# W_up for four pairs at a time by a two-level bilinear scheme of 49 block products, gate and lora_A as extra columns, part of the weight operands streamed

## The chip, the cores and the metric

The kernel runs on one core of a Trainium2 chip. TensorE (PE) multiplies matrices and writes into PSUM; VectorE (DVE) and ScalarE (ACT) read and write PSUM and SBUF; GpSimd (POOL) works in SBUF; SyncE (SP) only issues transfers here. The metric is the device time of one execution in microseconds (us), the median over several runs. Everything is float32.

## The reference

x has 128 samples of 64 channels by 1024. Two layers each add a branch to x:

```python
def _L0_cond_ref(x, embedding, ...):          # a 64x64 mix of the channels, its weights chosen per sample
    att = softmax(mlp(embedding)); agg_w = einsum('bk,koi->boi', att, weight); agg_b = att @ bias_k
    return einsum('boi,bih->boh', agg_w, x) + agg_b[:, :, None]
def _L0_ffn_ref(x, A, B, bias):               # rank 128
    return einsum('bsd,od->bso', x, A @ B.T) + bias
def _L1_cond_ref(x, c, weight, c_weight, bias):   # grouped convolution, 9 taps, 4 groups, plus a context
    return conv(x, weight) + (c @ c_weight.T)[:, :, None] + bias[None, :, None]
def _L1_ffn_ref(x, W_up, gate_w, expert_bias, lora_A, lora_B):
    top1 = argmax(x @ gate_w.T + expert_bias)                 # 4 experts
    z = einsum('nh,erh->ner', x, lora_A)                      # rank 8
    delta = the chosen expert's einsum('ner,ehr->neh', z, lora_B)
    return x @ W_up.T + delta                                 # W_up is 1024 x 1024
x = x + _L0_ffn_ref(_L0_cond_ref(x, ...), ...)
x = x + _L1_ffn_ref(_L1_cond_ref(x, ...), ...)
```

The change is about the last function: the product with W_up (8192 rows by 1024 by 1024), the gate and z.

## The kernel before

Two samples make a pair: 128 rows (partitions) of 1024. There are 64 pairs. The order of the instructions on every engine is the order of the program text.

- Layer 0 per pair: `layer0_in` (xt times B, 8 calls, line 401), `layer0_mix` (the sample's mix, lines 411 and 419), `layer0_out` (two matmuls of 512 columns, line 432, added to x by DVE, line 433). x then goes through DRAM (`x1d`) into the tile X, which holds it turned for the convolution.
- Convolution per pair: POOL makes differences of X (lines 469 and 470), `shared_in` (line 477) and `conv_in` (line 515) multiply, `shared_out` and `conv_out` (lines 492, 495, 527) add the context and write `yt`, which is the turned input of the W_up product: 8 blocks of 128 columns of the 1024 for each of the two pairs.
- W_up, two pairs at a time: the product is cut into 2 row blocks (pairs) x 4 x 4 blocks of 256, which would be 32 block products. A bilinear scheme does it with 26. `ffn_sums` has POOL make 17 sums of parts of yt (line 216). `products` runs the 26 block products (line 559): each is two matmul calls, 128 x 128 by 128 x 256, onto half of one of four PSUM banks `pb`. Between them, ACT and DVE copy, add or evict parts of these banks (lines 564 to 578), as the table `PRODUCTS` says. All 26 weight operands lie in SBUF (`W`), made at the start from W_up by 31 sums (`w_sums`, on DVE with ACT copies to PSUM, and POOL).
- Gate and lora: `gate_in` multiplies yt by gate_w and lora_A (16 calls, line 586), the result is transposed (line 598), `gate` picks the expert on DVE (lines 601 to 612), `turn` transposes the masked z (line 622), `lora` adds z times lora_B onto the four open banks (line 631), and `results` adds the banks to x (line 637) and stores the pair.
- The main loop runs over d, two pairs, 32 times. In it the products of d stand between layer 0 and the convolution of later pairs. Loads of x and xt are issued by POOL (lines 157 and 161), all other steady transfers by SP.

Of the kernel before, what the change touches and what calls it, by code (L numbers as in the profile page):

```python
# [45 lines left out]
NG = NPAIR // GP  # L46
# [9 lines left out]
QC = NC // 4  # L56
# [3 lines left out]
GT = 64  # L60
NX = 3
NBD = 3
# [3 lines left out]

Y_SUMS = (  # L70
    (4, "+", 5), (0, "-", 8), (9, "+", 1), (2, "-", 10), (4, "-", 7), (0, "-", 12), (3, "-", 13),
    (2, "+", 14), (6, "-", 15), (16, "-", 5), (12, "-", 15), (17, "-", 18), (11, "-", 8), (20, "-", 19),
    (21, "+", 7), (7, "-", 13), (21, "+", 3),
)
W_SUMS = (
    (10, 8, "-", 10), (16, 10, "-", 6), (17, 4, "n", 16), (2, 2, "-", 6), (18, 11, "-", 15),
    (19, 18, "n", 16), (3, 3, "n", 15), (20, 1, "-", 3), (21, 7, "-", 20), (21, 5, "n", 21), (18, 8, "+", 18),
    (1, 5, "-", 1), (5, 9, "-", 10), (10, 6, "+", 20), (10, 5, "+", 10), (20, 12, "+", 2), (22, 4, "-", 3),
    (23, 5, "-", 13), (7, 4, "+", 7), (24, 3, "+", 2), (24, 0, "-", 24), (9, 9, "-", 13), (25, 12, "-", 18),
    (0, 0, "-", 4), (0, 12, "+", 0), (4, 14, "-", 23), (4, 2, "+", 4), (13, 13, "+", 21), (11, 11, "-", 21),  # L80
    (11, 8, "+", 11), (12, 14, "-", 12),
)
PRODUCTS = (
    (2, 6, 8, 1, 0, (("copy", 0, "-"),)),
    (4, 10, 17, 1, 3, (("x", 4, "+"),)),
    (6, 11, 16, 1, 3, (("copy", 1, "+"),)),
    (2, 12, 2, 0, 4, (("x", 6, "+"),)),
    (6, 2, 19, 0, 6, (("add", 0, "+"),)),
    (5, 8, 3, 0, 7, (("add", 4, "-"),)),
    (3, 17, 21, 0, 10, (("x", 7, "+"), ("x", 1, "+"))),  # L90
    (0, 15, 18, 0, 11, (("x", 7, "+"),)),
    (5, 5, 1, 0, 12, (("x", 7, "-"),)),
    (7, 8, 10, 0, 15, ()),
    (7, 19, 5, 0, 15, (("x", 1, "+"), ("x", 5, "+"))),
    (2, 13, 20, 0, 16, (("x", 2, "+"),)),
    (1, 20, 6, 0, 16, (("x", 2, "-"),)),
    (4, 9, 22, 0, 17, (("add", 2, "-"),)),
    (6, 18, 15, 0, 17, (("copy", 7, "-"), ("copy", 3, "-"))),
    (1, 21, 23, 0, 18, (("copy", 6, "-"),)),
    (4, 1, 7, 0, 19, (("x", 1, "-"), ("x", 3, "+"))),  # L100
    (2, 0, 24, 0, 21, (("dcopy", 4, "+"), ("x", 0, "+"))),
    (6, 22, 9, 0, 22, (("x", 5, "-"),)),
    (0, 14, 25, 0, 23, (("copy", 2, "+"),)),
    (4, 23, 0, 0, 25, ()),
    (6, 7, 4, 0, 27, ()),
    (1, 10, 10, 0, 27, ()),
    (1, 24, 13, 0, 28, ()),
    (7, 16, 11, 0, 30, ()),
    (2, 3, 12, 0, 31, ()),
)  # L110
NW = 26
ON_POOL = (16, 19, 20, 21, 23, 24, 27, 28)
LAST = ((21, 2), (24, 0), (25, 3), (26, 1))
# [5 lines left out]
def block(ctx: ExitStack, tc: tile.TileContext, a: dict, out: bass.AP):  # L119
    nc = tc.nc  # L120
    const = ctx.enter_context(tc.tile_pool(name="const", bufs=1))
    xpool = ctx.enter_context(tc.tile_pool(name="xpool", bufs=8))
    xtp = ctx.enter_context(tc.tile_pool(name="xtp", bufs=3))
    ps = ctx.enter_context(tc.tile_pool(name="ps", bufs=4, space=PSUM))
    psb = ctx.enter_context(tc.tile_pool(name="psb", bufs=1, space=PSUM))
# [3 lines left out]
    bcp = ctx.enter_context(tc.tile_pool(name="bcp", bufs=3))  # L129
    z0p = ctx.enter_context(tc.tile_pool(name="z0p", bufs=2))  # L130
    cvp = ctx.enter_context(tc.tile_pool(name="cvp", bufs=1))
    ytp = ctx.enter_context(tc.tile_pool(name="ytp", bufs=2))
    sp = ctx.enter_context(tc.tile_pool(name="sp", bufs=2))
    sums = ctx.enter_context(tc.tile_pool(name="sums", bufs=1))
# [18 lines left out]
    xs, xts, bds, aggbs, ctxs = {}, {}, {}, {}, {}  # L153

    def load_turned(pr, eng):
        xts[pr] = xtp.tile([P, NC, P], F32, tag="xt", name=f"xt{pr}")
        eng.dma_start(xts[pr], a["xt"][pr])

    def load_rest(pr, eng):
        xs[pr] = xpool.tile([P, L], F32, tag="x", name=f"x{pr}")  # L160
        eng.dma_start(xs[pr], a["x"][pr])

    def load_x(pr, eng=nc.gpsimd):
        load_turned(pr, eng)
        load_rest(pr, eng)

# [7 lines left out]
    pk = const.tile([P, PK[-1]], F32, name="pk")  # L174
    nc.sync.dma_start(pk[:, : PK[4]], a["pk"][:, : PK[4]])
    nc.sync.dma_start(pk[:, PK[4] :], a["pk"][:, PK[4] :])
    condT, w0, b0, b1, w1, w2, b2, cwT, fs, ebias = (pk[:, f:t] for f, t in zip(PK, PK[1:]))
# [3 lines left out]
    nc.scalar.activation(warm, warm, AF.Gelu)  # L181
    bk = loaded("bias_k", [8, CH])
# [4 lines left out]
    W = const.tile([P, NW, QC, NQ], F32, name="w")  # L187
    wdone = [0]

    def load_w(k, eng):  # L190

        eng.dma_start(W[:, 4 * k : 4 * k + 4].rearrange("p j c n -> p (j c n)"), a["wq"][k])

    def w_sums(upto, aside=True):

        for k in range(wdone[0], upto):
            to, x, op, y = W_SUMS[k]
            fresh = [W_SUMS[j][0] for j in range(max(k - 2, 0), k)]
            if op != "-" and x in fresh:
                x, y = y, x  # L200
            first = W[:, x]
            if k in ON_POOL:
                combine(nc.gpsimd, W[:, to], first, op, W[:, y])
                continue
            if aside and x not in fresh:
                first = bank(f"pw{k}")
                nc.scalar.copy(first, W[:, x].rearrange("p c n -> p (c n)"))  # L207
                first = first.rearrange("p (c n) -> p c n", c=QC)
            combine(nc.vector, W[:, to], first, op, W[:, y])
        wdone[0] = max(wdone[0], upto)  # L210

    def combine(eng, to, x, op, y):
        if op == "n":
            eng.scalar_tensor_tensor(to, x, -1.0, y, ALU.mult, ALU.subtract)
        else:
            eng.tensor_tensor(to, x, y, ALU.add if op == "+" else ALU.subtract)  # L216
# [10 lines left out]
    ones = const.tile([P, P], F32, name="ones")  # L227
# [10 lines left out]
    aggd = dram.tile([NB, CH, CH], F32, name="aggd")  # L238
    ctxd = dram.tile([NB, CH], F32, name="ctxd")
# [23 lines left out]

    def mlp(w, h, b, name):
        p = bank(f"p{name}")
        nc.tensor.matmul(p[:, :NB], w, h, start=True, stop=True)
        o = const.tile([P, NB], F32, tag=name, name=name)
        nc.scalar.activation(o, p[:, :NB], AF.Gelu, bias=b)
        return o

    def spare(j, name):

        return psb.tile([P, N], F32, tag=f"pb{j}", name=name)
# [6 lines left out]
    def condition():  # L280
# [18 lines left out]
        nc.vector.reciprocal(rs, sm)  # L299
        nc.vector.tensor_scalar(att[:, :, :8], ex.unsqueeze(1).to_broadcast([P, 4, 8]), rs, None, ALU.mult)  # L300
# [6 lines left out]
    def b_row():  # L307

        p = spare(2, "pbs8")
        for c in range(NC):  # L310
            nc.tensor.matmul(p[:8, :P], ones[:, :8], bt[:, c], start=c == 0, stop=c == NC - 1)
        nc.scalar.copy(bs8, p[:8, :P])
# [16 lines left out]
    def own_bias(pr):  # L329

        mv[pr] = sums.tile([8, 2, CH], F32, tag=f"s{10 + pr}", name=f"mv{pr}")
        for b in range(2):
            nc.scalar.activation(mv[pr][:, b], bk, AF.Copy, scale=attT[:8, 2 * pr + b : 2 * pr + b + 1])

    def own_bd(pr):
        bdx[pr] = sums.tile([P, 2, CH], F32, tag=f"s{14 + pr}", name=f"bdx{pr}")
# [28 lines left out]
    def agg_all():  # L365

        to = aggd.rearrange("b i o -> b (i o)").rearrange("b (j h n) -> h b j n", j=4, h=2)
        for h in range(2):
# [4 lines left out]
            else:  # L373
                whole = W[:, NW - 4 :].rearrange("p j c n -> p j (c n)")
# [19 lines left out]
    xbs, z0s, yts, opened = {}, {}, {}, {}  # L394
    diffs, pms, m2s, pcs, zgs, ys = {}, {}, {}, {}, {}, {}
# [10 lines left out]
    def layer0_mix(pr):  # L406
        g, t = pr // GP, pr % GP
        own = pr < FIRST
        pz = bank(f"pz{pr}")
        bd = bdx[pr] if own else bds[g][:, t]  # L410
        nc.tensor.matmul(pz[:, :P], xbs.pop(pr), bd.rearrange("p b o -> p (b o)"), start=True, stop=not own)  # L411
# [3 lines left out]
        if own:  # L415
# [122 lines left out]

    def ffn_sums(d, first=0, end=len(Y_SUMS)):

        if not first:
            ys[d] = [yts[d][:, t, QC * k : QC * (k + 1)] for t in range(2) for k in range(4)]
        y = ys[d]
        for k, (u, op, v) in list(enumerate(Y_SUMS))[first:end]:
            y.append(sums.tile([P, QC, P], F32, tag=f"s{k}", name=f"s{k}_{d}"))
            combine(nc.gpsimd, y[-1], y[u], op, y[v])

    def part(d, r):
        return opened[d][r // 2][:, r % 2 * NQ : (r % 2 + 1) * NQ]

    def products(d, first, end):
        if not first:
            opened[d] = [psb.tile([P, N], F32, tag=f"pb{i}", name=f"pb{i}_{d}") for i in range(4)]
        for r, u, w, new, _, then in PRODUCTS[first:end]:
            p = part(d, r)
            if new == 2:
                nc.vector.memset(p, 0.0)
            for c in range(QC):
                nc.tensor.matmul(  # L559
                    p, ys[d][u][:, c], W[:, w, c], start=new == 1 and c == 0, stop=c == QC - 1, skip_group_check=True  # L560
                )
            for kind, to, op in then:
                if kind == "dcopy":
                    nc.vector.tensor_copy(part(d, to), p)
                elif kind == "copy" and op == "+":
                    nc.scalar.copy(part(d, to), p)
                elif kind == "copy":
# [231 lines left out]
    for d in range(NPAIR // 2):  # L799
# [8 lines left out]
        if d:  # L808
            zm = gate(d)
# [135 lines left out]
```

## Time and profile before

| | |
|---|---|
| median of 3 runs | 1276.93 us (1276.56 to 1277.66) |
| span of the profiled execution | 1275.4 us |
| PE busy | 1256.2 us, 98% |
| POOL, DVE, ACT busy | 731.1 us 57%; 698.4 us 55%; 233.2 us 18% |
| matmul instructions | 9255 |
| transfers | 189.72 MB, mean 149 GB/s; HBM read 118.90 MB, written 69.27 MB |
| SP's queue, POOL's queue, ACT's queue | 126.07 MB, 35.8% of 16 engines; 58.73 MB, 13.8%; 3.41 MB, 0.8% |
| share of the ending chain by line 559 (products) | 55% |

The profile is one execution, whose own time is the span. Busy time of PE counts instructions that overlap; the distance from one start to the next is the time that one takes of the engine. A float32 matmul call leaves two records.

### The profile page before, as it was taken

To read this page: it belongs to the slowest core of one execution; us is meant where nothing else is said; L and a number is where in the kernel's file an instruction comes from. 1 tells how busy PE (TensorE), PEld (TensorE's weight loads), DVE (VectorE), ACT (ScalarE), POOL (GpSimd) and SP (SyncE) were. 2 spreads that over 40 slices of the span, in tenths; PEclk is the share of its full clock that TensorE was granted. 3 is DMA by queue.
4 is the path that set the end of the run, shared out by engine and by line. 5 is a ranking of instruction groups with operands and counts; after the bars stand their busy time and mean duration, and the time that the engine had idled before them with its cause. 6 is when DMAs were issued, how large, how long until landed. Compare 5 with 4: busy or idle time off the path is not lost.

```text
span 1275.4 us, 23721 instructions
## 1 busy us (share of the span) xinstructions
PE 1256.2 (98%) x9255; PEld 1057.1 (83%) x9255; DVE 698.4 (55%) x1477; ACT 233.2 (18%) x586; POOL 731.1 (57%) x868
## 2 busy tenths in 40 slices
PE   8989999999999999999999999999999999999998
PEld 6768888888888888888888888888888888888886
DVE  6666545546545456555455555455555465455454
ACT  3321121111111111111211111111111111211111
POOL 2475676555576455676555676555775555765332
PEclk9989999999999999999999999999999999999999
DMA  9965444565444565444664444664444654445301
GB/s 307 341 164 160 147 136 115 147 176 163 135 131 111 165 176 161 140 118 110 176 176 149 143 110 128 176 174 143 137 109 141 176 171 135 137 113 149 104 34 67
DMA packets 184159, 189.72 MB, mean 149 GB/s; under 512 B 17392, under 2 KB 156656, under 8 KB 183536
## 3 DMA queue, kind: packets, MB, share of 16 engines
q1 hardware_dynamic: 166912, 126.07, 35.8%
q0 software_dynamic: 16128, 58.73, 13.8%
q10 hardware_dynamic: 1008, 3.41, 0.8%
q8 instruction: 74, 1.21, 0.4%
q14 instruction: 37, 0.30, 0.1%
HBM read 118.90 MB, written 69.27 MB: 148 GB/s over the span
## 4 chain that ended last, share of the span: by engine, by line
PE 93%; DMA 4%; DVE 1%; ACT 1%; issue 0%; SPq 0%; POOL 0%; DVEq 0%; POOLq 0%; ACTq 0%
PE pb L559 55%; PE pxb L401 9%; PE pd L432 8%; PE pc L515 8%; PE pm L477 4%; PE pg L586 4%; PE pb L631 3%; DMA w<-in_wq 1%; DMA x1d<-x 1%; PE pz L411 1%; DMA aggd<-agg 1%; DMA X<-x1d 1%; DMA ffn_bias<-in_ffn_bias 1%; ACT pw L207 0%; DVE yt L527 0%
## 5 line engine op out<-in xcount | busy, mean ns | idle before, releaser
L559 PE MATMUL pb<-w,s 128*128 128x256 f32 x2432 | 558.3, 380 | 6.0 <-DVE w L216 4.5
L559 PEld LDWEIGHTS pb<-w,s 128*128 128x128 f32 x2432 | 460.4, 191 | 72.1 <-DVE w L216 4.9
L469 POOL TENSOR_TENSOR df<-X 128x512 f32<-128x512 f32 x62 | 64.1, 1034 | 387.8 <-DMA X<-x1d 387.8
L559 PE MATMUL pb<-w,yt 128*128 128x256 f32 x896 | 225.6, 380 | 2.3 <-DVE x L637 1.8
L492 DVE TENSOR_TENSOR m<-pm,cx 64x512 f32<-64x512 f32 x124 | 85.3, 688 | 203.0 <-PE pm L477 196.4
L559 PEld LDWEIGHTS pb<-w,yt 128*128 128x128 f32 x896 | 162.9, 190 | 31.5 <-issue 8.7
L576 DVE TENSOR_TENSOR x<-pb,x 128x256 f32<-128x256 f32 x320 | 129.2, 421 | 95.6 <-PE pb L559 88.9
L216 POOL TENSOR_TENSOR s<-yt,s 128x256 f32<-128x256 f32 x224 | 165.6, 739 | 17.8 <-PE pb L559 2.8
L656 POOL TENSOR_TENSOR x<-x,ffn_bias 128x1024 f32<-128x1024 f32 x61 | 142.7, 2355 | 17.0 <-DMA x<-in_x 17.0
L401 PEld LDWEIGHTS pxb<-B,xt 128*128 128x128 f32 x1024 | 118.7, 194 | 25.1 <-DVE yt L527 22.0
L527 DVE TENSOR_TENSOR yt<-pc,m 128x512 f32<-128x512 f32 x124 | 122.6, 1112 | 25.0 <-ACT m L495 19.4
L401 PE MATMUL pxb<-B,xt 128*128 128x128 f32 x1024 | 124.6, 280 | 0.2 <-DMA xt<-in_xt 0.2
L432 PE MATMUL pd<-AT,z 128*128 128x512 f32 x256 | 121.3, 595 | 2.6 <-DVE attx L327 1.6
L515 PE MATMUL pc<-ws,df 128*64 128x128 f32 x1984 | 113.6, 273 | 0.0
L515 PEld LDWEIGHTS pc<-ws,df 128*64 128x64 f32 x1984 | 109.4, 137 | 0.0
L433 DVE TENSOR_TENSOR x<-pd,x 128x512 f32<-128x512 f32 x128 | 88.2, 691 | 37.4 <-PE pd L432 30.1
L571 ACT COPY v<-pb 128x256 f32<-128x256 f32 x96 | 35.8, 372 | 371.7 <-PE pb L559 352.9
L216 POOL TENSOR_TENSOR s<-s,yt 128x256 f32<-128x256 f32 x128 | 93.5, 731 | 15.7 <-PE pzt L622 8.3
L495 ACT COPY m<-m 64x512 f32<-64x512 f32 x124 | 76.6, 618 | 134.1 <-DVE m L492 124.5
L216 POOL TENSOR_TENSOR s<-s,s 128x256 f32<-128x256 f32 x128 | 92.2, 730 | 5.0
L578 DVE SCALAR_TENSOR_TENSOR x<-pb,x 128x256 f32<-128x256 f32 x128 | 54.0, 422 | 68.1 <-PE pb L559 66.6
L637 DVE TENSOR_TENSOR x<-pb,x 128x512 f32<-128x512 f32 x124 | 76.8, 683 | 8.7 <-PE pb L631 8.7
(107 smaller groups left out, 915.3 us busy)
## 6 DMA issues: line engine op xcount, KB each, us to landing
x1d<-x SPq DMA_DIRECT2D x128, 256.0 KB, 4.4
X<-x1d SPq DMA_DIRECT2D x128, 256.0 KB, 4.3
out<-x SPq DMA_DIRECT2D x62, 512.0 KB, 3.6
xt<-in_xt POOLq DMA_DIRECT2D x56, 512.0 KB, 6.0
x<-in_x POOLq DMA_DIRECT2D x56, 512.0 KB, 6.5
cx<-ctxd SPq DMA_DIRECT2D x32, 128.0 KB, 4.3
w<-in_wq SPq DMA_DIRECT2D x4, 1024.0 KB, 12.4
ab<-aggbd SPq DMA_DIRECT2D x30, 128.0 KB, 3.4
```

The lines of the kernel that those rows point to most:

```text
L216: eng.tensor_tensor(to, x, y, ALU.add if op == "+" else ALU.subtract)
L401: nc.tensor.matmul(pxb[:, :P], xt[:, c, :], bt[:, c, :], start=(c == 0), stop=(c == NC - 1))
L432: nc.tensor.matmul(pd, z0, at[:, cols], start=True, stop=True)
L433: nc.vector.tensor_tensor(x[:, cols], pd, x[:, cols], ALU.add)
L492: nc.vector.tensor_tensor(by_group(m2[half, b]), by_group(pm[half]), context(pr, b, half), ALU.add)
L495: nc.scalar.copy(m2[other, b], m2[half, b])
L515: nc.tensor.matmul(pc[o * H : (o + 1) * H, cols], diffs[pr][:, 2 * g + b, o], ws[:, g, o], start=True, stop=True,)
L527: nc.vector.tensor_tensor(yt.rearrange("m q (o g two) -> m two g q o", two=2, g=NGC)[:, b], by_group(pcs.pop((pr, b))), context(pr, b) if ...
L559: nc.tensor.matmul(p, ys[d][u][:, c], W[:, w, c], start=new == 1 and c == 0, stop=c == QC - 1, skip_group_check=True)
L576: nc.vector.tensor_tensor(x, p, x, ALU.add)
L637: nc.vector.tensor_tensor(x[:, cols], b, x[:, cols], ALU.add)
L656: eng.tensor_tensor(xs[pr], xs[pr], fbias, ALU.add)
```

## The change

W_up is now done for four pairs at a time, 16 times. Four pairs are two "rows" r of two pairs. The product is cut into 2 x 2 x 2 large blocks, which a bilinear scheme of 7 products handles (`Outer`, i = 0 to 6: operand sums `OPERANDS`, destinations `DESTS`). Each of the 7 is again cut into 2 x 2 x 2 and done with 7 products, in a form whose sums are chained (`inner`, `rest`). So there are 49 block products of two calls each, where 64 would be the plain number.

- Operands on the left: `gather` makes one sum of 1024 elements for five of the seven outers, `inner` makes four sums of 256 for each, all on POOL.
- Operands on the right: four of each outer's seven are held in SBUF (28); the other three (21 in all) are written to DRAM at the start (`w_store`) and fetched again for each group of four pairs (`w_fetch`, 768 KB, on ACT's queue) into a ring of two buffers.
- Gate: for outers 0 to 3 the held operands are 292 columns wide; the 36 last columns are gate_w and lora_A, brought through the same scheme. ACT copies these columns out of PSUM (`gated`), `gate` adds them up. The matmuls of `gate_in` and one transpose are gone.
- PSUM: one bank `pa` and a ring of three banks `pt` in place of the four `pb`. Every outer's results are evicted at once onto x, to one or two places.
- `lora` writes four banks of its own, which DVE adds to x.
- x for two pairs lies in one tile (4 tiles in place of 8), loaded and stored by transfers of 1 MB. All loads are issued by SP; POOL issues none. Buffers change: 2 BD in place of 3, 2 context buffers in place of 3, 3 yt in place of 2, and a 1024-byte scratch for POOL's transfers.
- The start is written out anew: the operands are formed by `w_block` and `w_late` between the first four pairs' products.

```diff
-Y_SUMS = (
...
-PRODUCTS = (
...
+DESTS = (
+    ((0, 1, "+"), (1, 1, "+")),
+    ((0, 0, "-"), (0, 1, "+")),
+    ((0, 0, "+"), (1, 0, "+")),
+    ((1, 0, "+"), (1, 1, "-")),
+    ((0, 0, "+"), (1, 1, "+")),
+    ((0, 0, "+"),),
+    ((1, 1, "+"),),
+)
+OPERANDS = (
+    ((0, 0),),
+    ((0, 0), "+", (0, 1)),
+    ((1, 1),),
+    ((1, 0), "+", (1, 1)),
+    ((0, 0), "+", (1, 1)),
+    ((0, 1), "-", (1, 1)),
+    ((1, 0), "-", (0, 0)),
+)
...
+    def w_fetch(i):
+        nc.scalar.dma_start(ring_tile(i).rearrange("p k c n -> p (k c n)"), wd[i])
...
+        def gather(self):
+            o = OPERANDS[self.i]
+            if len(o) == 1:
+                self.S = self.operand(*o[0])
+                return
+            self.S = sums.tile([P, GP, 4, P], F32, tag="S", name=f"S{self.name}")
+            combine(nc.gpsimd, self.S, self.operand(*o[0]), o[1], self.operand(*o[2]))
...
+        def product(self, p, lhs, w, fresh=False):
+            for c in range(2):
+                nc.tensor.matmul(p, lhs[:, c], w[:, c], start=fresh and c == 0, stop=c == 1, skip_group_check=True)
...
+        def first(self):
+            self.t1 = pst.tile([P, N], F32, tag="pt", name=f"ta{self.name}")
+            self.product(self.t1[:, : self.n], self.unit(0, 0), held(self.i, 0), True)
+        def spread(self):
+            self.pa = psa.tile([P, N], F32, tag="pa", name=f"pa{self.name}")
+            nc.scalar.copy(self.pa[:, :NQ], self.t1[:, :NQ])
+            self.gated(2, self.t1)
+        def rest(self, then, hooks):
+            self.t2 = pst.tile([P, N], F32, tag="pt", name=f"tb{self.name}")
+            wt = WT[self.i]
+            self.product(self.t2[:, :NQ], self.s[0], wt[:, 1], True)
+            v = tmp.tile([P, NQ], F32, tag="v", name=f"v{self.name}")
+            nc.scalar.copy(v, self.t2[:, :NQ])
+            hooks("a")
+            self.product(self.pa[:, :NQ], self.s[1], wt[:, 2])
+            nc.scalar.copy(self.t2[:, :NQ], self.pa[:, :NQ])
+            hooks("b")
+            self.product(self.t1[:, : self.n], self.unit(0, 1), held(self.i, 1))
+            self.gated(0, self.t1)
+            self.evict(self.t1[:, :NQ], 1)
+            hooks("c")
+            self.product(self.pa[:, :NQ], self.s[3], wt[:, 0])
+            hooks("d")
+            self.product(self.t2[:, : self.n], self.s[2], held(self.i, 2))
+            nc.scalar.copy(self.pa[:, NQ:], self.t2[:, :NQ])
+            both = self.pa.rearrange("p (k n) -> p k n", k=2)
+            combine(nc.vector, both, both, "+", v.unsqueeze(1).to_broadcast([P, 2, NQ]))
+            self.evict(both, 3)
+            if then:
+                then.first()
+            self.product(self.t2[:, : self.n], self.unit(1, 1), held(self.i, 3))
+            if then:
+                then.spread()
+            self.gated(1, self.t2)
+            self.evict(self.t2[:, :NQ], 2)
...
+    for d in range(1, ND):
...
+        w_fetch(1)
+        if more:
+            load_cond(r0)
+            load_cond(r1)
+            load_rows_of(r0)
+            load_turned(pairs(r1)[0])
+        q[1].gather()
+        q[1].inner()
+        if more:
+            for pr in pairs(r0):
+                add_fbias(pr, nc.gpsimd)
+        q[0].rest(q[1], nothing)
+        if more:
+            in_rows(r0)
...
+        w_fetch(6)
+        if more:
+            load_context(r1)
+        q[6].gather()
+        q[6].inner()
+        q[5].rest(q[6], nothing)
+        lora(d, 1, zts[1])
+        store(d, 0)
+        if more:
+            w_fetch(0)
+            for pr in pairs(r1):
+                differences(pr)
+            o[d + 1, 0].gather()
+            o[d + 1, 0].inner()
+        q[6].rest(o[d + 1, 0] if more else None, nothing)
+        store(d, 1)
+        if more:
+            conv_rows(r1)
```

The parts left out of the loop stand in the same manner: outer 1, then `out_rows(r0)`; outer 2, then `in_rows(r1)` and `lora(d, 0)`; outer 3, then `out_rows(r1)`; outer 4, then `conv_rows(r0)`. The fetch for outer k + 1 always stands before the `rest` of outer k.

## The prediction, made before the changed kernel was run

> **What bounds the kernel now.** I read four views in this order: the engines over 40 slices, the chain of work that ended last, TensorE's timeline over one period, and the groups of instructions.
>
> ```profile
> PE   8989999999999999999999999999999999999998
> PEclk9989999999999999999999999999999999999999
> ...
> PE 93%; DMA 4%; DVE 1%; ACT 1%; issue 0%; SPq 0%; POOL 0%; DVEq 0%; POOLq 0%; ACTq 0%
> 610.60:649.20 38.60, 38.60 (x288) 32.66 (x287) 20.85 (x45) 6.73 (x17) 22.97 (x27) 1.00 0.51 147
> ```
> TensorE (PE) works without a gap at full granted clock from about 100 to 1200 us. The last line is one period, two pairs in 38.53 us: PE 100%, VectorE (DVE) 20.85 us, ScalarE (ACT) 6.73, GpSimd (POOL) 22.97, DMA share 0.51. So a change is worth the PE time it removes, as long as no other engine or transfer becomes late.
>
> ```profile
> 594.45 1.97 PE L477 MATMUL pm<-wsum,X 128*64 128x128 f32 x32
> 596.25 1.92 PE L586 MATMUL pg<-yt,gl 128*64 128x128 f32 x32
> 597.99 3.66 PE L515 MATMUL pc<-ws,df 128*64 128x128 f32 x64
> 601.59 1.14 PE L631 MATMUL pb<-lb,zt 32*128 32x512 f32 x8
> 602.66 3.84 PE L401 MATMUL pxb<-B,xt 128*128 128x128 f32 x32
> ...
> 610.01 1.88 PE L432 MATMUL pd<-AT,z 128*128 128x512 f32 x4
> 611.73 0.38 PE L411 MATMUL pz<-bd,xb 128*128 128x128 f32 x2
> ...
> 617.40 12.95 PE pb L559 x60
> ```
> The first seven lines are the timeline (start, us), the last is from the chain. PE overlaps its instructions, so a price is the distance from one start to the next: pm 1.80 for two pairs, gate pg 1.74, convolution pc 3.60, lora 1.07, pd 1.72 per pair (4 records of 512 columns, 430 ns each). A block product's record of 256 columns costs 12.95/60 = 215.8 ns. Each matmul call leaves two records.
>
> ```profile
> L576 DVE TENSOR_TENSOR x<-pb,x 128x256 f32<-128x256 f32 x320 | 129.2, 421 | 95.6 <-PE pb L559 88.9
> L433 DVE TENSOR_TENSOR x<-pd,x 128x512 f32<-128x512 f32 x128 | 88.2, 691 | 37.4 <-PE pd L432 30.1
> L527 DVE TENSOR_TENSOR yt<-pc,m 128x512 f32<-128x512 f32 x124 | 122.6, 1112 | 25.0 <-ACT m L495 19.4
> L571 ACT COPY v<-pb 128x256 f32<-128x256 f32 x96 | 35.8, 372 | 371.7 <-PE pb L559 352.9
> L656 POOL TENSOR_TENSOR x<-x,ffn_bias 128x1024 f32<-128x1024 f32 x61 | 142.7, 2355 | 17.0 <-DMA x<-in_x 17.0
> q0 software_dynamic: 16128, 58.73, 13.8%
> out<-x SPq DMA_DIRECT2D x62, 512.0 KB, 3.6
> aggd<-w SPq DMA_DIRECT2D x1, 1024.0 KB, 5.9
> x<-in_x ACTq DMA_DIRECT2D x1, 512.0 KB, 11.0
> ```
> These are prices of the small work that the new scheme adds, and of transfers.
>
> **The change, on PE, per four pairs (two old periods, 77.06 us).** 52 calls per two pairs become 98 per four: 208 records become 196, so 12 x 0.2158 = -2.59. The gate matmuls go: 2 x 1.74 = -3.48; with them two transposes pgt at 0.11 = -0.22. Added: 4 of the 7 outer products carry 36 extra columns in 4 of their 7 inner ones, 4 x 4 x 2 calls x 2 = 64 records. From 256 to 512 columns a record grows 215.8 to 430 ns, 0.84 ns a column, so 30 ns each: +1.92. Lora and its transposes keep their number. Net -4.37: **a new period of 72.7 us**.
>
> **What must stay hidden, per new period.** DVE: 24 evictions of 256 columns x 0.421 = 10.1, 12 of 512 x 0.69 = 8.3, 7 sums in PSUM x 0.69 = 4.8, lora 8 x 0.68, pd 8 x 0.69, yt 8 x 1.11, m 8 x 0.69, z 1.4, two gates of ten small operations, 4: together 54 us against 41.7. POOL: 5 gathers of 1024 elements x 2.36, 28 sums x 0.74, bias 9.4, differences 8.3: 50 us against 46. ACT: 28 copies x 0.37, 12 gate copies of 36 columns (about 0.25, as zg), m, xb, zt: 20 us, and 7 fetches to issue. All are below 72.7.
> The order matters more than the sums. I walked one period by hand, T = 0 at the first inner product of outer 0. PE: outers 0 to 2 6.52 each (3 x 0.863 + 4 x 0.983), outer 3 6.40, 4 and 5 6.04, 6 6.16; between them stand in order in_rows 3.8, out_rows 3.4, in_rows and lora 4.8, out_rows 3.4, convolution 5.4, lora 1.1, convolution 5.4. The tightest circle inside an outer runs from its fifth product: ACT copy 0.37, DVE sum 0.69, two evictions 1.38, ACT spread 0.37, then the next outer's second product may start: 2.8 us with hops of some 0.04 (DVE w ended at 68.46, PE began at 68.50). PE has 0.98 + 0.98 + 0.86 = 2.8 us of its own there plus the work in between, at least 1.07. Hidden. If DVE runs late there, the delay shows one to one. POOL finishes each outer's sums 6 us or more before use, because their two buffers come free one outer earlier.
>
> **The streamed operands.** 105 fetches (15 periods x 7) of 768 KB on ACT's queue, 82.6 MB, and 5.5 MB of stores. q0 moved 58.73 MB in 13.8% of the span, 334 GB/s, so this takes 264 us more of all 16 engines: share 0.51 to about 0.75. A fetch is issued by ACT between its copies; it blocks nothing long, since its ring buffer is already free. From issue to the matmul that needs it I count 6.7 us (outer 6: issued after the m copies, covered by outer 5 and lora alone), then 10.0 (1), 10.2 (2), 11 (4), 12.4 (0), 14.8 (3), 14.9 (5). Price of landing, not in the trace for this size: below, between 512 KB in 3.6 and 1024 KB in 5.9, so 4.7; above, the 512 KB load on ACT's queue that took 11.0 while the DMA share was near 1. I take near the lower end, 5 to 6, because the share is 0.75 and the packets are long; 0.3 us a period is put in for bad cases, 4 us in all.
> The Trainium skill speaks against taking ACT's queue as a path of its own: "DMA: Bandwidth & Descriptors", section "Issuing engines are not separate DMA queues", says all queues run on the same 16 engines and interleave. If SP's queue takes every second turn, the fetch needs its 2.4 us at 334 GB/s twice: 7.1 instead of 4.7, so 0.4 late for outer 6, 6 us over 15 periods, in place of my 4.
> All x and xt loads move from POOL's to SP's queue, where they queue with x1d, X, stores and conditions: 32 issues of about 0.55 = 18 us per period, and X and x have 10 us or more to spare in my walk. POOL loses its issues and its wait for `out<-x` (41.1 us in all), which cost PE nothing.
>
> **The start.** Before, lora of the second period ends at 139.2. The changed kernel reaches the same point (eight pairs convolved, four finished) at: 44.2 (pd of pair 3, as before) + 79.0 of PE work (seven outers 45.2, three convolution groups 16.2, the rest 17.6) = 123.2 without a wait. I expect waits of 12.8: 1.4 for W's first block (4 DVE steps behind ACT copies), 1.0 in its first outers, 4.3 where outer 3's gather waits for four yt sums and then POOL's 2.36, 0.5 there, 4.0 where lora wants PSUM banks while DVE still works off block 2 and pd, 1.6 in outer 3 to 5. So 136. Bounds: 123 with none, 149 with twice as many.
>
> **The end.** The last period has no new pairs: 72.7 less 26.1 of in, mix, out and convolution, less 0.98 = 45.6; without work between outers the circle above shows at four places, 1.5 in all. After the last matmul: eviction 0.42, then one store of 1 MB (5.9) instead of 256 KB pieces: 6.5 against some 4 before.
>
> **Sum.** 136 + 14 x 72.7 + 45.6 + 1.5 + 4 + 6.5 = 1211.4 us of span. The profile before had 1275.4, the median of the runs 1276.93, so 1.5 lie around it: **1213 us**, a factor of 0.950.
>
> **Rivals.**
> (a) *The gain is there, half is eaten by short waits per period*: DVE, 54 us in 72.7 and in strict order, is late in the circle or with PSUM banks (lora wants four at once), or the start takes 149. For it: in the walk DVE has hardly a pause from T = 12 to 29 and 43 to 58, and margins of 1 us. Against: no step of the walk is late. With 2 us a period, 28, and 10 at the start: about 1250.
> (b) *The fetches become the bound, slower than before.* A landing time of L costs (L - 6.7) + (L - 10.0) + (L - 10.2) a period. The gain of 64 us is gone at 4.3 us a period, from L = 10.4. For it: the 11.0 above, and 12.4 for 1 MB in the start. At 11.0 it is 6.1 a period, 92 us: about 1305. Against: both rows lie where the DMA share was 0.9 to 1.0; in the steady part, loads of 512 KB on a queue of their own took 6 to 6.5 even behind one another.
> (c) *The gate columns save nothing*, if 36 columns more cost as much as a record of 128 (118 ns): 64 x 0.118 = 7.6 instead of 1.9, 5.6 x 16 = 90 us, 1303. Two records of a matmul with 256 and 512 columns lie on one line, so I give this little.
>
> **Chances.** Forecast 0.66 (its own range 1201 to 1226), (a) 0.22, (b) 0.09, (c) 0.03. A measurement of this kernel can tell 0.2%, 2.6 us. Faster: the forecast and (a), less a tail: 0.87; within 0.2%: 0.02; slower: 0.11. The range 1201 to 1255 takes the forecast and most of (a).
>
> **What would show it.** The changed period: 72.7 us with 196 records for the products, 64 of them near 246 ns; no idle PE there. Idle PE in front of products that read the streamed tiles would be (b), with fetches landing above 10 us; idle in front of the second product of an outer, released by ACT, would be (a). A start that reaches the fourth convolution group later than 149, or DVE busy above 85% in a period, would make the prediction wrong.

## The result, and the profile after

| | before | after |
|---|---|---|
| median | 1276.74 us (1275.59 to 1277.66, 4 runs) | 1414.38 us (1409.36 to 1414.79, 4 runs) |
| span of the profiled execution | 1275.4 us | 1413.0 us |
| PE, DVE busy | 98%, 55% | 89%, 71% |

The ratio is 1.1068 (95% interval 1.1045 to 1.109): slower by a tenth, where a gain of 5% was forecast, and outside the range. The page of after, the rows that answer to those of before (busy shares, slices, the chain by engine):

```profile
PE 1253.7 (89%) x8007; PEld 994.8 (70%) x8007; DVE 1004.8 (71%) x1670; ACT 316.8 (22%) x928; POOL 784.6 (56%) x746
...
PE   8879899898997979979899898989989899798997
...
PEclk9989989999999989999999999999999999999999
...
PE 53%; issue 14%; DVE 11%; POOL 10%; DMA 8%; SPq 1%; ACT 1%; ACTq 0%; DVEq 0%; POOLq 0%
```

PE now has dips all along the span, and DVE and POOL stand in the chain, where they had 1% and 0%. 1248 matmul records are gone, yet the end comes later. One new period, from one `in_rows` to the next but one (columns: length; busy us of PE, weight load, DVE, ACT, POOL; clock; DMA share; GB/s):

```profile
616.10:701.47 85.37, 76.67 (x496) 61.00 (x495) 60.73 (x99) 18.20 (x54) 48.73 (x45) 0.96 0.63 196
```

85.4 us instead of the 72.7 of the prediction: PE is idle for 8.7 us and the mean granted clock is 0.96. In the kernel before, PE was busy for all of the 38.60 us of a period (two pairs). Where PE stands still is in its timeline (start, us, then the wait and its releaser in brackets):

```profile
601.43 1.03 PE L645 MATMUL pa<-wt,s 128*128 128x256 f32 x4
602.29 1.15 PE L645 MATMUL ta<-wg,yt 128*128 128x292 f32 x4
609.45 0.48 PE L736 MATMUL pzt<-ident,zm 128*128 128x128 f32 x1 [6.01 <-DVE xr L505]
609.72 1.91 PE L645 MATMUL pa<-wt,s 128*128 128x256 f32 x4
611.43 2.15 PE L645 MATMUL tb<-wg,s 128*128 128x292 f32 x4
613.38 1.90 PE L645 MATMUL ta<-wg,S 128*128 128x292 f32 x4
```

The transpose `pzt` of `turn` needs a PSUM bank that `pd` still holds, since DVE has not yet added `pd` to x (L505). The products behind it then take about 1.9 us in place of 1.03 to 1.15: the granted clock from 609.72 to 616.10 is 0.59. The same place one row later (637.10) waits 2.72, and here the products behind it stay at 1.03. That is not so in every period: behind five of the 14 waits of this second kind the clock fell too, as behind the one that ended at 203.97:

```profile
609.72:616.10 6.38, 6.38 (x18) 4.69 (x18) 4.11 (x8) 0.62 (x2) 1.88 (x3) 0.59 0.71 171
637.10:642.00 4.90, 4.90 (x39) 4.21 (x41) 4.77 (x10) 0.91 (x3) 1.66 (x2) 1.00 0.57 163
204.00:209.00 5.00, 5.00 (x16) 4.13 (x17) 4.26 (x8) 0.62 (x2) 0.60 (x1) 0.66 0.54 161
```

What made DVE late, on DVE and below it on POOL:

```profile
601.25 0.45 DVE L718 TENSOR_TENSOR sc<-lg,mx 128x8 f32<-128x8 f32 x1
601.74 2.28 DVE L719 TENSOR_TENSOR sc<-sc,rank 128x8 f32<-128x8 f32 x1
604.05 0.16 DVE L721 TENSOR_REDUCE ms<-sc 128x2 f32<-128x8 f32 x1
604.24 2.07 DVE L723 TENSOR_TENSOR oh<-sc,ms 128x8 f32<-128x8 f32 x1
606.34 2.46 DVE L726 TENSOR_TENSOR zm<-pv,oh 128x64 f32<-128x64 f32 x2
608.72 2.47 DVE L505 TENSOR_TENSOR xr<-pd,xr 128x512 f32<-128x512 f32 x4
```
```profile
601.64 4.65 POOL L755 TENSOR_TENSOR xr<-xr,ffn_bias 128x1024 f32<-128x1024 f32 x2
606.24 2.34 POOL L204 TENSOR_TENSOR S<-yt,yt 128x1024 f32<-128x1024 f32 x1
```

An operation on 8 columns takes 2.28 us. In the kernel before, the same operations took 0.165 to 0.175; this is the row that answers to L719 (busy us, mean ns):

```profile
L605 DVE TENSOR_TENSOR pgt<-pgt,rank 128x8 f32<-128x8 f32 x32 | 5.6, 174 | 1.1
```

L719 ends at 604.02, and POOL's first bias addition (half of 4.65) at 603.97; L723 ends at 606.31, POOL's second at 606.29; the pair L726 at 608.80, the gather at 608.58. The maximum L721 between them, which reads one tensor, stays at 0.16. So an operation of the gate with two inputs in SBUF ends when POOL's running instruction does. In the kernel before, `lg` and `sc` were parts of the PSUM bank `pgt`; the change has no such bank any more and put them, and the sums `pv`, into SBUF. The two gates (from 599.20 and from 630.28, to DVE's next work) last 9.5 and 6.1 us; I had 2 for each.

The Trainium skill says this, and I had not applied it: "SBUF — State Buffer", section "Who interferes with whom": a VectorE instruction with two inputs in SBUF contends with a GpSimd instruction that reads SBUF, the one that comes second is blocked while the other's instruction lasts, and a reduction never contends on this chip. The rows above agree: 2.28 beside POOL's 2.33, and 0.16.

Of 201.6 us between the span and the sum of the prediction (1211.4), 182 are 14 periods, each 13.0 longer than the 73.0 of the sum (72.7, and 0.3 for the fetches); 11.3 are the start, 9.0 the last period, and -0.8 the tail. The 13.0 can be split with the same 14 periods of the kernel without waits, the best one below (first line after, second line that kernel, both from the first product behind the start to the last period):

```profile
147.35:1351.19 1203.84, 1077.49 (x6918) 859.74 (x6916) 855.97 (x1387) 254.88 (x756) 687.67 (x635) 0.95 0.63 194
146.47:1175.83 1029.36, 1029.36 (x6919) 831.40 (x6917) 694.41 (x1415) 261.30 (x784) 686.83 (x636) 1.00 0.77 227
```

Per period, 9.0 are the two waits (126.4 us in 28). 3.4 are the low clock: for the same products PE is busy 48 us longer, 2.6 of the 3.4 behind the longer wait in the period shown (6.38 us for four products that take 3.8 at full clock). The last 0.5 stand in the kernel without waits too: its period is 73.5.

### The profile page after: what moved, and what is told of

It reads as the page before. It is cut to its first block, busy times and chain, and to the rows that moved or that the text cites. A ratio compares the mean times of both kernels' runs of the same rounds, so it can differ in the third digit from the quotient of the medians.

```text
span 1413.0 us, 22026 instructions
## 1 busy us (share of the span) xinstructions
PE 1253.7 (89%) x8007; PEld 994.8 (70%) x8007; DVE 1004.8 (71%) x1670; ACT 316.8 (22%) x928; POOL 784.6 (56%) x746
## 3 DMA queue, kind: packets, MB, share of 16 engines
q8 instruction: 65, 1.06, 0.3%
## 4 chain that ended last, share of the span: by engine, by line
PE 53%; issue 14%; DVE 11%; POOL 10%; DMA 8%; SPq 1%; ACT 1%; ACTq 0%; DVEq 0%; POOLq 0%
PE tb L645 15%; PE pa L645 10%; PE ta L645 8%; PE pc L587 7%; PE pxb L473 4%; PE pm L549 4%; POOL s L204 4%; DMA xt<-in_xt 3%; DVE xr L204 2%; POOL df L541 2%; POOL df L542 2%; PE pl L746 2%; DVE oh L723 2%; DMA xr<-in_x 2%; DVE sc L719 1%
## 5 line engine op out<-in xcount | busy, mean ns | idle before, releaser
L204 POOL TENSOR_TENSOR S<-yt,yt 128x1024 f32<-128x1024 f32 x48 | 113.1, 2357 | 263.7 <-PE tb L645 198.1
L645 PE MATMUL pa<-wt,s 128*128 128x256 f32 x896 | 244.8, 398 | 1.1 <-ACT zs L652 1.1
L755 POOL TENSOR_TENSOR xr<-xr,ffn_bias 128x1024 f32<-128x1024 f32 x61 | 142.0, 2348 | 172.1 <-DMA xr<-in_x 149.3
L645 PEld LDWEIGHTS pa<-wt,s 128*128 128x128 f32 x896 | 173.7, 200 | 30.9 <-issue 3.4
L204 POOL TENSOR_TENSOR s<-S 128x256 f32<-128x256 f32 x160 | 116.5, 728 | 61.2 <-PE tb L645 56.0
L736 PE MATMUL pzt<-ident,zm 128*128 128x128 f32 x32 | 12.7, 396 | 139.0 <-DVE xr L505 126.4
L204 DVE TENSOR_TENSOR xr<-xr,pa 128x512 f32<-128x512 f32 x192 | 124.8, 684 | 3.8
L645 PE MATMUL tb<-wt,s 128*128 128x256 f32 x448 | 121.6, 394 | 0.0
L748 DVE TENSOR_TENSOR xr<-pl,xr 128x512 f32<-128x512 f32 x128 | 79.4, 682 | 54.3 <-PE pl L746 54.2
L645 PEld LDWEIGHTS tb<-wt,s 128*128 128x128 f32 x448 | 78.7, 190 | 49.8 <-issue 36.8
L204 DVE TENSOR_TENSOR xr<-xr,tb 128x256 f32<-128x256 f32 x192 | 73.5, 417 | 44.4 <-ACT zs L652 42.7
L645 PE MATMUL ta<-wp,S 128*128 128x256 f32 x384 | 102.9, 392 | 0.0
```

The costliest lines, as they stand in the source:

```text
L645: nc.tensor.matmul(p, lhs[:, c], w[:, c], start=fresh and c == 0, stop=c == 1, skip_group_check=True)
L748: nc.vector.tensor_tensor(x, p, x, ALU.add)
L755: eng.tensor_tensor(xs[pr], xs[pr], fbias, ALU.add)
```

## The experiments

Theory A: the gate's operations in SBUF wait for POOL's long instructions, DVE comes late to `pd`, PE waits. Rivals: DVE is simply short of time, or the transposes stand too early, or the fetches bind. The kernel before took 1276.5 to 1276.7 beside each of them.

**The gate's operands back in PSUM.**

```diff
-        pv = sp.tile([P, 3, GL], F32, tag="pv", name=f"pv{d}_{r}")
-        nc.vector.tensor_tensor(pv, zs[:, 0], zs[:, 1], ALU.add)
...
+        pt = bank(f"pgt{d}_{r}")
+        pv = pt[:, : 2 * GL].rearrange("p (t c) -> p t c", t=2)
+        lg, sc = (pt[:, P + k * 2 * E : P + (k + 1) * 2 * E].rearrange("p (t e) -> p t e", t=2) for k in range(2))
+        nc.scalar.copy(pv, zs[:, 0, :2])
+        nc.vector.tensor_tensor(pv, pv, zs[:, 1, :2], ALU.add)
+        nc.vector.tensor_tensor(pv[:, 1], pv[:, 1], zs[:, 0, 2], ALU.add)
+        nc.vector.tensor_tensor(pv[:, 1], pv[:, 1], zs[:, 1, 2], ALU.add)
```

> The changed kernel with the gate's intermediates (pv, lg, sc) in a PSUM bank, so that no DVE operation of the gate reads two SBUF tiles; ACT copies 72 columns into the bank first, and the two sums become three. Theory A (the gate's small DVE operations wait for POOL's instructions because both their operands come from SBUF; everything behind them on DVE is late, and the transpose pzt waits for the bank that pd's additions hold): the ten operations fall from 6 to 9.5 us to about 2.2, PE's waits of 6.0 and 2.7 us before pzt go, and with them the slow clock after them; period 72.7 to 74, time 1215 to 1235. Theory B (DVE simply has too much work, 54 us in 72.7, and the ring of four banks makes pzt wait for pd in any case): the gate's operations get shorter by little, the waits stay, time above 1350.

Measured: 1289.26 us (1287.74 to 1289.44), ratio 1.0095 (1.0078 to 1.0112). 125 us come back, but not all that was expected. L719 and its neighbours are at 0.17 us again, a gate lasts 2.3, and the waits at `pzt` are gone from the loop. A new one is there (waits: engine, line and releaser, us in total, times, longest):

```profile
PE pd L504 <- DVE zm L727: 48.2, 28, 1.7
```

The gate's new bank is the fourth of four, so the fourth `pd` matmul waits until the gate has done. That is from my edit, 48 of the 54 to 74 us that were missed; others lie in the start, whose fourth convolution group ends at 144.6 where 136 was forecast.

**Only the transposes moved back**, behind the work that stands after each outer; gate in SBUF as in after.

```diff
-        q[2].rest(q[3], hook({"c": [turn0]}))
+        q[2].rest(q[3], nothing)
         if more:
             in_rows(r1)
+        turn0()
```

(the same for `turn1`, behind `conv_rows` and `back`)

> The gate as in the changed kernel (SBUF), only the transpose pzt and its copy are moved later on PE and ACT: behind in_rows and behind the convolution, some 7 to 9 us later. Theory A: DVE is as late as before, the gate's operations stay long, but PE meets pzt after the bank is free; of the 13.3 us that a period is over 72.7, the wait of 6.0, that of 2.7 and the slow clock go, some 11 to 12 us; what is left of DVE's lateness shows before the lora or before an outer's second product; 1413 less 14 x 11.5 = about 1250, between 1230 and 1280. Theory B: the lateness is work, not waiting, so it reappears as another wait of the same size: above 1350.

Measured: 1351.42 us (1350.04 to 1352.7), ratio 1.0585 (1.0569 to 1.06). My range for theory A is missed, and the time lies just inside that of theory B (above 1350). The gate's operations stay long (L719 1265 ns on average), and DVE's lateness shows in other places: 36.4 us at `pxb` behind L505, 32.9 at `pc` behind the context additions. Another 17.7 at `pl` are from the edit: lora waits for ACT's copy of the transposed z, which now comes right before it. Moving the wait is not removing it; by itself this run does not tell theory A from a DVE that is short of time, and speaks rather for the latter.

**The kernel before with its gate's scratch in SBUF.**

```diff
-        lg, sc = (pt[:, P + k * 2 * E : ...] for k in range(2))
+        lg, sc = (sp.tile([P, 2, E], F32, tag=f"gs{k}", name=f"gs{k}_{d}") for k in range(2))
```

> The kernel before, with lg and sc of its gate in SBUF in place of PSUM; nothing else. Theory A: its operations with two SBUF operands (is_equal, times rank, is_equal: 0.17 us each) grow to between 0.5 and 2 us each where POOL works beside them, up to POOL's longest instruction (2.36); the sum and the two maxima, which read at most one SBUF tile, stay at 0.17. The time stays within 0.5% of the kernel before, since its transpose comes 13 us after the gate. Theory B: all stay at 0.17.

Measured: 1281.45 us (1276.78 to 1283.62, 10 runs), ratio 1.0035 (1.0023 to 1.0048). It says little: in that kernel's loop POOL is idle while the gate runs (618.3 to 619.5; POOL starts again at 624.55, after a wait for X). One gate in the start fell beside a POOL instruction: its `gs<-gs,rank` took 2.28 us, next to a bias addition of 2.36 us that had begun 0.1 us earlier. So the same placement left the operations at 0.17 us where POOL's order left the moment free. The median is 5 us above the kernel before, clear of the noise; the one long operation is 2 of them at most, the profiled run (1277.59) was among the two shortest of the ten, and where the rest comes from is not shown.

**The first experiment without the fetches.** `w_fetch` reuses the ring's last tiles.

> The kernel of e1 without the 105 fetches of streamed operands: the products of later periods read the ring's last two tiles again, so those parts of W_up are wrong in the result. My term for the fetches was 0.3 us a period (4 us in all), with 92 us if they land after 11 us. If the fetches are hidden, the time is that of e1 within 5 us; if they cost something, it is lower by that.

Measured: 1290.12 us, one run, against 1289.26. 105 fetches of 768 KB cost nothing that can be measured there.

**POOL's long instructions in quarters**, gate in SBUF, order as in after: the test of how the two engines meet.

```diff
-        eng.tensor_tensor(xs[pr], xs[pr], fbias, ALU.add)
+        w = L // 4
+        for s in (slice(k * w, (k + 1) * w) for k in range(4)):
+            eng.tensor_tensor(xs[pr][:, s], xs[pr][:, s], fbias[:, s], ALU.add)
```

(the gathers likewise)

> The changed kernel with GpSimd's long additions (the gathers of 1024 elements and the bias, 2.35 us each) cut into four of 256 elements; the gate's operands stay in SBUF, the order stays. GpSimd's own work grows by about 0.6 us for each, 9 a period. Theory A (a small VectorE operation with two SBUF operands waits for the end of GpSimd's running instruction, so the longest GpSimd instruction sets the longest wait): no gate operation takes above 1.1 us (the differences are 1.04), L719's mean falls from 1363 ns to 400 to 800, gate(d,0) from 9.5 us to 5 to 6.5, the waits in front of pzt from 6.0 + 2.7 to 2 to 5 in all, and the time to 1300 to 1355. Rival B (the two engines share a path byte by byte, and an operation is slowed in proportion): cutting changes nothing, L719's mean stays above 1100 ns, and the time stays within 15 us of 1414.

Measured: 1311.56 us (1307.73 to 1320.95), ratio 1.0285 (1.0239 to 1.0331): 103 us less than after, with more work on POOL (844 us busy instead of 785). The groups of after, then of this kernel (busy us, mean ns):

```profile
L719 DVE TENSOR_TENSOR sc<-sc,rank 128x8 f32<-128x8 f32 x32 | 43.6, 1363 | 1.1
L723 DVE TENSOR_TENSOR oh<-sc,ms 128x8 f32<-128x8 f32 x32 | 35.9, 1122 | 1.1
L721 DVE TENSOR_REDUCE ms<-sc 128x2 f32<-128x8 f32 x32 | 5.2, 161 | 1.1
```
```profile
L723 DVE TENSOR_TENSOR sc<-sc,rank 128x8 f32<-128x8 f32 x32 | 22.3, 696 | 1.1
...
L727 DVE TENSOR_TENSOR oh<-sc,ms 128x8 f32<-128x8 f32 x32 | 18.0, 564 | 1.1
...
L725 DVE TENSOR_REDUCE ms<-sc 128x2 f32<-128x8 f32 x32 | 5.1, 161 | 1.1
```

Both halve (the lines are four lower here: `sc<-sc,rank` is L723), no operation of this period's gates takes above 0.96 us, the gates last 5.2 and 5.8, and the waits at `pzt` are 1.65 and 2.41. The same bytes moved on POOL, so it isn't a path that is shared byte by byte: the length of POOL's single instruction sets the wait.

**Gate behind `out_rows`** (on the kernel with the gate in PSUM), so that `pd` takes its four banks first.

```diff
-        zms[0] = gate(d, 0)
         if more:
             out_rows(r0)
+        zms[0] = gate(d, 0)
```

> e1_gate_psum with one change: in the steady loop gate(d,0) and gate(d,1) stand behind out_rows, so that the four pd matmuls take their banks first and the gate takes the bank that the first pd addition gives back. Theory A (with its operands in PSUM the gate takes 2.3 us, and the 1.71 and 1.74 us that PE waits at the fourth pd matmul are only the gate's hold on the fourth bank): the two waits go, pzt waits at most 0.6 us each, the period falls from 77.46 to 74.0 to 74.6, 14 periods of 3.0 to 3.4 us less: 1289 - 45 = about 1243 us (1235 to 1255), faster than before. Rival B (VectorE is short of time over the whole period, as in e2_turn_late, and its lateness reappears behind the gate): the period stays above 76.5 and the time above 1270.

Measured: 1257.14 us (1255.29 to 1258.02), ratio 0.9843 (0.9821 to 0.9864). The wait at `pd` is gone, and the kernel is faster than before by 1.6%. It is 2 us over the range; `pzt` waits 0.64 us for the gate on average, 30 times (19.1 us).

**And the transposes one product later.**

```diff
-        q[2].rest(q[3], hook({"c": [turn0]}))
+        q[2].rest(q[3], hook({"d": [turn0]}))
```

> e6_gate_after_pd, with the transposes pzt one product later in outers 2 and 4. Theory A: what e6_gate_after_pd still waits in front of pzt (at most 0.6 us each) goes, so 0 to 1.2 us a period and 0 to 17 us in all: 1230 to 1245. Rival B: as for e6_gate_after_pd, above 1270, since the wait reappears at the lora banks or at the next outer.

Measured: 1232.25 us (1230.62 to 1234.11), **ratio 0.9653 (0.9632 to 0.9674)**: the change's scheme, 182 us faster than after and 44 faster than before. It gained 25 us where at most 17 were expected: 19.1 are the waits at `pzt`, the rest was not split. One period, in the same columns as above:

```profile
604.88:678.40 73.52, 73.52 (x496) 59.39 (x495) 49.61 (x102) 18.66 (x56) 46.73 (x44) 1.00 0.76 228
```

PE is busy for all of 73.52 us at full clock, with the 496 records that after had. DVE is busy 49.61 instead of 60.73. The run also settles a rival that the first experiment left open: that the edit only moved the gate away from POOL's long instructions. Here a whole gate (609.34 to 611.67) stands beside the two bias additions, and its operations keep their 0.17 us:

```profile
609.06 4.68 POOL L756 TENSOR_TENSOR xr<-xr,ffn_bias 128x1024 f32<-128x1024 f32 x2
610.49 0.17 DVE L719 TENSOR_TENSOR pgt<-pgt,mx 128x8 f32<-128x8 f32 x1
610.70 0.17 DVE L720 TENSOR_TENSOR pgt<-pgt,rank 128x8 f32<-128x8 f32 x1
611.11 0.17 DVE L724 TENSOR_TENSOR oh<-pgt,ms 128x8 f32<-128x8 f32 x1
```

L724 has one input in PSUM and one in SBUF, and writes to SBUF: one input in PSUM is enough.

**The order alone**, gate in SBUF: the other corner.

> The changed kernel with the order of e7_turn_at_d alone (gate behind out_rows, pzt one product later); the gate's operands stay in SBUF. Theory A: the operations keep their lengths (L719 above 1000 ns on average, a gate 6 to 9.5 us), so pzt now waits for zm instead of for the bank, and the next evictions wait behind the gate: 1370 to 1425, about the changed kernel's 1414. Rival (the order alone was the fault and the place of the operands matters little): below 1270.

Measured: 1405.27 us (1401.39 to 1408.5), ratio 1.1001 (1.0968 to 1.1033). The time is as theory A says, one detail is not: L719 falls to 277 ns on average. Other operations have taken its place, on DVE and on POOL:

```profile
593.80 2.42 DVE L710 TENSOR_TENSOR pv<-zs 128x108 f32<-128x108 f32 x1
596.25 2.22 DVE L711 TENSOR_TENSOR pv<-pv 128x36 f32<-128x36 f32 x1
598.50 2.23 DVE L715 TENSOR_TENSOR lg<-pv,ebias 128x8 f32<-128x8 f32 x1
...
601.57 0.17 DVE L719 TENSOR_TENSOR sc<-sc,rank 128x8 f32<-128x8 f32 x1
```
```profile
593.73 4.68 POOL L755 TENSOR_TENSOR xr<-xr,ffn_bias 128x1024 f32<-128x1024 f32 x2
598.38 2.33 POOL L204 TENSOR_TENSOR S<-yt,yt 128x1024 f32<-128x1024 f32 x1
```

The gate stands at another moment, so POOL's three long instructions meet L710, L711 and L715: one operation passes per POOL instruction (ends at 596.22, 598.47, 600.73; POOL's second and third at 598.41 and 600.71). Which line is long is chance of position; that some are is the rule. `pzt` waits 6.29 and 2.58 for `zm`.

**Without the 36 columns**, on the best kernel (`w[:, c, :NQ]`, 256 columns everywhere).

> e7_turn_at_d without the 36 extra columns: all block products run with 256 columns and the gate works off the first 36 columns of the products in place of its own (gate and lora_A's products are left out, so the gate's choice and lora's part of the output are wrong). All else stays. The prediction's term says 64 records x 30 ns = 1.92 us a period, 16 periods: 31 us less than e7_turn_at_d. Rival (c) says 118 ns a record, 7.6 us a period: 121 us less. If PE is not the bound: less than 15.

Measured: 1207.82 us (1206.57 to 1208.13), 24.4 less than with the columns, 1.5 for each group of four pairs where the term was 1.92. Rival (c) falls.

**Without the fetches**, on the best kernel.

> e7_turn_at_d without the 105 fetches (the ring's two last tiles are reused for all outers, so parts of W_up's product are wrong). All else stays. If the stream is hidden, as the prediction says: 0 to 5 us less (its 4 us for bad cases). Rival (b), the fetches bind now that TensorE has hardly an idle moment: more than 15 us less.

Measured: 1233.4 us (1231.84 to 1235.26), against 1232.25. The stream is hidden also where PE has no idle moment; the DMA share is 0.76 there. Rival (b) falls.

## Why the prediction was wrong

- **The step that failed**: "two gates of ten small operations, 4" in the list of what must stay hidden, with "no step of the walk is late" resting on it. They take 9.5 and 6.1 us. The price, 0.2 us an operation, fits the rows of the kernel before (0.17 to 0.22), whose operands lay in PSUM, and the change had moved them to SBUF. The text of the prediction speaks of every added operation, and of none whose operands change place. With operands in PSUM (and then the order) the same gate takes 2.3 and hides; with the order alone it does not. Both edits are needed to be faster than before: 1414 as changed, 1405 with the order, 1289 with PSUM, 1232 with both.
- **The circle that the walk left out**: DVE late, then `pd` not added, so no bank for `pzt`, then PE idle for 6 us, then half the clock for its next 6 us. My rival (a), "DVE ... is late in the circle or with PSUM banks", named the place, but at 2 us a period, a sixth of what came.
- **The PE work was right.** A period of 72.7 was forecast; the kernel without waits has 73.52. The 0.8 lie where kinds of matmul change, which I had left out: seven products a period take 0.96 to the next start instead of 0.87, and the lora right behind `in_rows` takes 1.47 instead of 1.07. The 16 products with gate columns take 0.98 instead of 0.86, which is the 1.92 of the sum; leaving the columns out gained 1.5.
- **DVE's 54 us a period were too many** for the kernel that I had in mind (49.61). My sign "DVE busy above 85%" did not warn: it was 71% with the waits. A sum over a period says nothing on which operation is late.
- **The fetches were right**: they landed in 5.8 us (median), within the 5 to 6 of the forecast and short of the 7.1 of strict turns with SP's queue, and cost nothing; the 4 us for bad cases were not needed.
- **The start was too short**: 136 forecast; 147.35 in after, 146.5 in the best kernel, inside the bounds of 123 to 149. There the listed idle times come to some 13 us, near the 12.8 that I had put in, the largest 6.46 in front of `pxb`, where DVE was late with a block of W's operands. The other 10 are in the 79.0 us of PE work: 2.8 of them are the low clock behind that wait (0.51 from 74.75 to 80.55), the rest is not split. How much of it can be won was not tried.
- **The best kernel against the sum** of 1211.4, without its 1.5: 1231.7, or 10.5 more in the start, 11.6 in 14 periods, 2.3 in the last period and the tail, and 4 less for the fetches. The size of the scheme's gain was forecast within 20 us; its sign was lost where the operands of two small gates lie.

## What to carry to other kernels

When a change moves the operands of a small VectorE operation from PSUM to SBUF, or drops the PSUM tile that held them, price the operation again: with two SBUF inputs, beside a busy GpSimd, each can last as long as GpSimd's longest instruction (2.3 us here), and several in a row can do so one after another. Walk the chain behind it to the next PSUM bank and the next matmul, and look at single durations beside the other engine's, not at busy shares. The cures, in the order of what they gave here, were operands in PSUM (125 us), shorter GpSimd instructions (103 us), and an order in which the bank is free before it is asked for (57 us, once the first was done).

## What the runs showed of the hardware

- A VectorE operation with both input tensors in SBUF ended with GpSimd's running instruction: 2.28 us for 8 columns beside additions of 2.33 us, up to 0.96 beside pieces of 0.7 to 1.0, 0.17 with one input in PSUM, also beside additions of 2.34. The reduction with one tensor kept 0.16 in all of them. GpSimd's own instructions kept their length (2.35 us).
- After 6.0 us of idle PE the granted clock was 0.59 over the next 6.4 us. After 2.7 us, in the kernel after, it stayed at 1.00 in nine of the 14 periods and fell in five (0.66 from 204.00 to 209.00); in the kernel with quarters it fell also behind a wait of 2.41 us (0.63 from 431.80 to 436.00). "TensorE: Matmul & The Clock Gate" of the Trainium skill, section "Part 1", names an idle window of about 3.4 us: the long waits agree, but these runs show that a shorter one does not keep the clock safe.
- With the fetches the DMA share in a period was 0.76; a kernel without them had the same time within 1.2 us.
